# A re-planned order for a graph layer: separate sums for pairs 12 and 13, and zero products that may go into banks about to be set

## The chip, the cores and the metric

The kernel runs on one core of one Trainium2 chip. The metric is the device time of one execution in microseconds (us); several runs of the same kernel give a median. A profile records one execution instruction by instruction; its span runs from the first to the last instruction and is a little shorter than the execution's own time.

## What is computed

A layer of a graph network with 4096 nodes and 64 features. The adjacency matrix, 4096 x 4096 float32 of zeros and ones (64 MB), is nearly all of the traffic.

```python
h = jnp.maximum(_layernorm(x, axis=-1), 0.0)
# _L0_gnn_ref(h, adj, weight, bias), with MAX_NEIGH = 100 and DECAY = 0.5:
support = input @ weight
mask = (adj != 0).astype(support.dtype)
rank = jnp.cumsum(mask, axis=1)
deg = rank[:, -1:]
k = jnp.minimum(deg, float(MAX_NEIGH))
pos = rank - (deg - k)
w = mask * jnp.where(pos > 0, DECAY ** (k - pos), 0.0)
out = w @ support + bias
# result: x + out
```

So a row's last neighbour weighs 1, the one before it 1/2, and so on for at most 100 neighbours: each entry's weight is two to the minus number of neighbours behind it in its row.

## The kernel before

The rows are cut into 32 tiles of 128 rows; a tile (128 x 4096, 2 MB) is also called a unit, and two tiles are a pair (`u`, 16 of them). All tiles go through the same steps:

- `load`: DMA from SP's queue into one of four buffers `a_sb`. The first two tiles and tiles 28 to 31 come in parts.
- `convert` and `flip` (DVE, L563 and L573): the mask as bytes, then a transposition in blocks of 32.
- `totals` (PE, L581, 8 products), `split` (ACT, L589), `suffix` (PE, L602, 9 products), `clamp` (DVE, L608): how many neighbours lie behind each block of columns.
- `place` (PE, L618 and L622, 24 products into four banks): the number of neighbours behind each entry, as an exponent.
- `weigh` (ACT, L636, four to a tile; tiles 29 and 31 in parts): the power of two. For one quarter of tiles 30 and 31 DVE does it instead (`encode` L643, `take` L647).
- `aggregate` (PE, L656): weights times `support`, for a pair of tiles, in eight steps of four products, 32 products in all, summed in a PSUM bank.
- `drain` (ACT L671 or DVE L673) takes the sums out of the bank and adds the bias; `turn_back` (PE, L679) transposes them; `finish` (DVE, L685) adds x; `store` writes.

Ahead of this there is a setup: layer norm and `support` (`turn` to `second`). It fills the first 40 us beside the first tiles.

A bank of sums holds two pairs: `aggregate` takes a new bank at an even pair, and at each pair in `ALONE` (L652). `DRAINS` lists the drains as (group of four tiles, first and last tile in it, whether ACT does it). Before, groups 0 to 6 are drained whole, six of them on ACT and group 6 on DVE; group 7 (pairs 14 and 15, in `ALONE`) in two halves. Half drains share one buffer, `acc_part`, whole ones another, `acc_sb`.

The order of all instructions is fixed by a planner (`plan`, L243), which keeps one queue for each kind of step and picks the next step by the due numbers in `DUE` (L50) and by costs written into `tasks`. It also gives every step its PSUM banks out of eight (`homes`), taking those that come free first, and says how many zero products PE is to run ahead of a step: where it foresees a gap on PE, it asks for products of a zero matrix (`junk`), to keep PE active.

`warm` (L482) issues them. They add zero to a bank of sums that is open: `idle` names its place. `aggregate` sets `idle` to the bank it sums in (L659), and `drain` empties it when that bank is the one drained (L668). While `idle` is empty, `warm` issues nothing. Before any sums exist, the target is a spare bank that each product sets anew. In the loop at the end (L695) `warm` is called ahead of setting `homes` and of the step itself. Each engine then runs its instructions in the planned order.

Of the kernel before, what the change touches and what calls it, by code (L numbers as in the profile page):

```python
# [40 lines left out]

PARTS = {29: ((0, 4), (4, 8)), 31: ((0, 4), (4, 6), (6, 8))}
QUICK = {(30, 3), (31, 3)}
DRAINS = [(g, 0, 4, g < 6) for g in range(7)] + [(7, 0, 2, False), (7, 2, 4, True)]
STORES = [(0, 0, 16), (1, 0, 12), (1, 12, 14), (1, 14, 16)]
NA, NM, NT, NW, BANKS = 4, 4, 4, 2, 8

ALONE = {14, 15}

DUE = {  # L50
    "fetch": [32, 37],
    "load": [35, 38, 39, 40, 36, 34, 33, 29, 31, 21, 20, 16, 25, 14, 18, 17, 15, 12, 13, 11, 6, 2, 1, 3, 7, 5, 9, 8, 4,
    0, 24, 22, 23, 19, 27, 28, 26, 30, 41, 64],
    "constants": [442, 424],
    "order_of": [427],
    "stack": [404],
    "turn": [483, 491, 461, 509, 470, 469, 515, 471],
    "turned": [435, 436, 438, 437, 434, 428, 431, 420],
    "center": [458, 447, 478, 432],
    "square": [441, 443, 492, 466],  # L60
    "relu": [439, 477, 482, 490],
    "spread": [473, 430, 460, 462],
    "support": [419, 97, 465, 459],
    "scale": [500, 454, 449, 507],
    "root": [452],
    "power": [495],
    "count": [474],
    "counted": [444],
    "first": [303, 326, 360, 309],
    "second": [501, 457, 503, 497],  # L70
    "convert": [426, 423, 425, 421, 453, 450, 448, 502, 499, 456, 498, 508, 510, 513, 514, 518, 529, 532, 522, 528, 629,
    631, 623, 626, 591, 617, 618, 538, 604, 594, 600, 553, 599, 593, 560, 584, 587, 564, 554, 578, 576, 570, 550, 551,
    546, 547, 609, 545, 611, 575, 607, 573, 574, 582, 561, 566, 614, 556, 637, 638, 654, 645, 656, 541, 552, 504],
    "flip": [429, 433, 446, 440, 455, 511, 496, 519, 517, 521, 523, 526, 624, 625, 619, 542, 592, 606, 559, 588, 563,
    586, 569, 548, 613, 622, 610, 572, 585, 565, 568, 557, 653, 641, 655, 648, 544, 493, 540, 534],
    "totals": [445, 418, 94, 112, 489, 84, 87, 138, 140, 144, 130, 118, 119, 208, 256, 229, 86, 221, 168, 228, 186, 165,
    145, 164, 197, 179, 49, 45, 63, 71, 73, 479],
    "split": [468, 298, 398, 367, 301, 306, 338, 385, 365, 389, 267, 369, 215, 291, 184, 201, 206, 274, 271, 261, 263,
    401, 335, 319, 295, 293, 322, 379, 381, 414, 356, 357],
    "suffix": [467, 463, 120, 111, 487, 139, 106, 141, 98, 126, 128, 107, 193, 207, 200, 157, 161, 174, 247, 250, 163,  # L80
    212, 205, 198, 177, 236, 55, 66, 69, 76, 51, 650],
    "clamp": [422, 451, 494, 506, 512, 516, 520, 527, 596, 627, 628, 616, 595, 601, 603, 598, 543, 589, 577, 579, 549,
    605, 621, 580, 571, 581, 562, 615, 652, 644, 597, 567],
    "place": [324, 464, 93, 142, 134, 133, 147, 105, 135, 103, 155, 191, 232, 75, 82, 151, 175, 213, 249, 223, 173, 237,
    169, 167, 180, 42, 65, 60, 79, 74, 481, 612],
    "weigh": [505, 216, 243, 342, 321, 325, 328, 361, 312, 307, 302, 355, 366, 387, 373, 374, 386, 364, 354, 399, 396,
    394, 362, 345, 392, 340, 384, 280, 390, 391, 284, 276, 242, 189, 265, 289, 375, 219, 241, 257, 292, 204, 255, 187,
    283, 297, 290, 190, 203, 211, 282, 270, 252, 259, 264, 268, 275, 244, 262, 269, 281, 287, 273, 285, 266, 246, 346,
    334, 279, 288, 327, 278, 332, 260, 402, 339, 337, 348, 314, 331, 341, 299, 351, 336, 311, 320, 310, 376, 308, 318,
    323, 315, 294, 316, 329, 317, 304, 248, 305, 330, 382, 417, 286, 296, 370, 406, 383, 388, 371, 393, 377, 416, 359,  # L90
    368, 350, 358, 378, 395, 352, 372, 405, 412, 397, 347, 353, 333, 349, 403, 413, 343, 415, 407, 410, 344, 411, 409],
    "encode": [533, 524],
    "take": [590, 525, 531, 536],
    "aggregate": [484, 115, 114, 110, 113, 109, 486, 488, 485, 124, 125, 123, 100, 91, 136, 132, 81, 121, 96, 127, 131,
    104, 129, 116, 95, 117, 108, 101, 122, 102, 152, 99, 92, 240, 188, 154, 89, 194, 199, 231, 183, 230, 220, 83, 90,
    85, 78, 77, 159, 153, 148, 150, 222, 158, 162, 166, 235, 214, 234, 245, 300, 182, 258, 227, 253, 225, 178, 195, 218,
    185, 224, 313, 192, 239, 202, 210, 254, 146, 143, 196, 160, 217, 176, 171, 181, 149, 172, 170, 209, 46, 47, 57, 48,
    43, 58, 56, 54, 62, 44, 88, 80, 68, 50, 70, 472, 52, 72, 480, 67, 475, 53, 651, 59, 476, 630, 660, 634, 632, 639,
    647, 657, 649, 658, 640, 642, 643, 633, 636],
    "drain": [363, 277, 251, 272, 400, 380, 608, 583, 408],  # L100
    "turn_back": [137, 233, 156, 226, 238, 61, 661, 659, 646],
    "finish": [530, 602, 558, 555, 620, 635, 537, 539, 535],
    "store": [662, 663, 664, 10],
}
WAIT = 250, 60, 150, 60, 0
PE, DVE, ACT, POOL, SP = range(5)
# [136 lines left out]
def plan():  # L243

    todo, kinds = tasks(), {}
    for key, (f, args, engine, *_) in todo.items():
        kinds.setdefault((engine, f), []).append(key)
    ready, free = {None: 0}, list(FREE)
    landed, taken, order = 0, {p: [] for p in SIZES}, []
    banks = [None] * (BANKS - 1) + read_by(0)  # L250
    while kinds:
        heads = []
        for kind, keys in kinds.items():
            f, args, engine, due, hold, lag, needs, pool = todo[keys[0]]
            if pool and pool[0] in SIZES:
                needs = needs + (taken[pool[0]] + list(pool[1:]))[:-SIZES[pool[0]]][-len(pool) + 1:]
            elif pool:
                needs = needs + [k for _, _, k in sorted((ready[k], i, k) for i, k in enumerate(banks) if k in ready)][:len(pool) - 1]
                if len(needs) < len(todo[keys[0]][6]) + len(pool) - 1:
                    continue  # L260
            if all(r in ready for r in needs):
                heads.append((max([free[engine]] + [ready[r] for r in needs]), due, engine, kind))
        soon, _, engine, _ = min(heads)
        _, at, kind = min((due, at, kind) for at, due, e, kind in heads if e == engine and at <= soon + WAIT[engine])
        key = kinds[kind].pop(0)
        if not kinds[kind]:
            del kinds[kind]
        f, args, _, _, hold, lag, _, pool = todo[key]
        homes = []
        if pool and pool[0] in SIZES:  # L270
            taken[pool[0]] += pool[1:]
        elif pool:
            homes = [i for _, i in sorted((ready[k], i) for i, k in enumerate(banks) if k in ready)][:len(pool) - 1]
            for i, k in zip(homes, pool[1:]):
                banks[i] = k
        if f in ("load", "fetch"):
            lag = max(landed - at, 2450) + dma_ns(f, args)
            landed = at + lag
            lag += late(landed)
        if f in FULL:  # L280
            hold, lag = hold + 95, lag + 95
        ready[key] = at + lag + 60
        free[engine] = at + hold
        order.append((at, hold, engine, f, args, homes))
    spent, end, result = [], 1200, []
    for at, hold, engine, f, args, homes in order:
        idle = 0
        if engine == PE:
            recent = sum(rows for when, rows in spent if when > at - 3400)
            idle = max(0, min(int((at - end) * 0.6) // 110, (4200 - recent) // 256))  # L290
            spent += [(at, rows_of(f, args) + 256 * idle)]
            end = at + hold
        result.append((at, idle, f, args, homes))
    return result
# [3 lines left out]
def kernel(  # L298
# [12 lines left out]
    nc = tc.nc  # L311
    P = 128
# [21 lines left out]
    banks = [ps.tile([P, W], F32, name=f"bank{i}") for i in range(BANKS)]  # L334
    homes = []
# [35 lines left out]
    junk = setup.tile([P, 2 * P], BF16, name="junk")  # L371
# [108 lines left out]
    idle = [banks[BANKS - 1], 2 * P]  # L480

    def warm(n):  # L482
        for i in range(n if idle else 0):
            nc.tensor.matmul(idle[0][:, idle[1]:idle[1] + 2 * P], junk[:, :P], junk, start=not accs, stop=not accs, skip_group_check=True)  # L484

    pxs, ns = {}, {}

# [199 lines left out]
    def store(s):  # L687
# [5 lines left out]
        support, scale, first, second, convert, flip, totals, split, suffix, clamp, place, weigh, encode, take, aggregate,  # L693
        drain, turn_back, finish, store)}
    for at, spare, f, args, given in plan():  # L695
        warm(spare)
        homes[:] = given
        does[f](*args)

    last = {}  # L700
# [34 lines left out]
```

## Time and profile before

| | |
|---|---|
| median of 3 runs | 186.7 us (185.85 to 187.02) |
| the profiled execution | 187.01 us, of which the span is 185.0 us |
| mean granted TensorE clock | 0.98 |
| PE (matmul) busy | 165.2 us (89%) |
| PE weight loads busy | 128.4 us (69%) |
| DVE busy | 153.9 us (83%) |
| ACT busy | 149.5 us (81%) |
| HBM read | 68.19 MB, 374 GB/s over the span |
| weigh (L636) on ACT | 122.7 us, 136 instructions |
| convert (L563) on DVE | 85.7 us, 66 instructions |
| products of aggregate (L656) on PE | 73.2 us, 512 instructions |
| zero products (L484) on PE | 14.7 us, 93 instructions |

The page gives sums over the whole span; three engines are above 80%. Matmuls overlap, so a mean duration of a product (292 ns for L656) is longer than the distance between two: 32 products in a row take about 4 us. A line of the timeline shows the start, the length, the engine, the line of the kernel, the operation with its output and input, how many instructions are merged, and in brackets how long the engine was idle before it and what it waited for. A line of the windows shows a stretch's length, each engine's busy time in it with the number of instructions, the granted TensorE clock (1.00 is full), the share of the DMA engines and GB/s.

### The profile page before, as it was taken

Reading aid. Unit: us, or ns where it says so; the run is one execution under the profiler, and the core shown is the slowest. Engines: PE = TensorE matmul, PEld = TensorE weight load, DVE = VectorE, ACT = ScalarE, POOL = GpSimd, SP = SyncE. Lnnn points to the kernel's source line nnn. Section 1 sums busy time; section 2 is a strip of 40 time slices with the busy share of each in tenths; the row PEclk is TensorE's granted clock in tenths of the full one; section 3 lists DMA queues with packets and bytes.
Section 4 is the critical chain, followed back from the end, with each engine's and each line's share of the span. In section 5 each row is a group of like instructions: output and inputs, shape, how many; then the busy total and the mean of one; then the engine's idle time right before and its main releaser. Section 6 shows DMA issues by size and latency. Waiting matters only on the chain.

```text
span 185.0 us, 4842 instructions
## 1 busy us (share of the span) xinstructions
PE 165.2 (89%) x2087; PEld 128.4 (69%) x2087; DVE 153.9 (83%) x204; ACT 149.5 (81%) x196; POOL 7.7 (4%) x43
## 2 busy tenths in 40 slices
PE   7999987579799999899999899997499999989992
PEld 5857874267586776687868588776277678777891
DVE  6667299999999999898889698888984989998731
ACT  2476912839699999999999999994896999999931
POOL 7810000000000000000000000000000000000000
PEclk9999999999999999999999999999958999999999
DMA  6999999999999999999999999999999999960020
GB/s 225 420 415 436 429 425 418 441 407 446 414 436 418 427 425 418 436 429 425 425 422 432 418 429 432 418 432 425 429 422 420 413 416 416 414 267 0 4 87 28
DMA packets 6807, 69.55 MB, mean 376 GB/s; under 512 B 898, under 2 KB 1154, under 8 KB 2178
## 3 DMA queue, kind: packets, MB, share of 16 engines
q1 hardware_dynamic: 6786, 69.24, 89.1%
q8 instruction: 16, 0.26, 0.6%
q14 instruction: 5, 0.04, 0.1%
HBM read 68.19 MB, written 1.05 MB: 374 GB/s over the span
## 4 chain that ended last, share of the span: by engine, by line
ACT 29%; PE 26%; DMA 19%; DVE 16%; issue 8%; SPq 0%; ACTq 0%; DVEq 0%
ACT wk L636 23%; DMA a_sb<-in_adj_dram 19%; PE bank L656 15%; DVE m L563 8%; ACT sums L589 4%; PE bank L602 4%; DVE mt L573 3%; PE bank L679 3%; PE bank L622 2%; PE bank L581 2%; PE bank L618 2%; DVE behind L608 1%; DVE wk L532 1%; DVE hr L542 1%; ACT acc_sb L671 1%
## 5 line engine op out<-in xcount | busy, mean ns | idle before, releaser
L636 ACT ACTIVATE wk<-bank 128x1024 fp32r<-128x1024 uint8 (+2 forms) x136 | 122.7, 1067 | 7.9 <-PE bank L622 6.3
L563 DVE TENSOR_SCALAR m<-a_sb 128x2048 uint8<-128x2048 f32 (+1 forms) x66 | 85.7, 1345 | 14.5 <-DMA a_sb<-in_adj_dram 14.3
L656 PE MATMUL bank<-wk,hr 128*128 128x256 f32 x512 | 73.2, 292 | 3.5 <-DVE hr L542 2.5
L656 PEld LDWEIGHTS bank<-wk,hr 128*128 128x128 f32 x512 | 64.4, 192 | 10.3 <-issue 5.0
L573 DVE STREAM_TRANSPOSE mt<-m 128x1024 f32<-128x1024 f32 (+2 forms) x40 | 40.5, 1022 | 0.4
L589 ACT ACTIVATE sums<-bank 128x512 f16<-128x512 uint8 x32 | 21.6, 685 | 7.2 <-PE bank L581 7.2
L608 DVE TENSOR_SCALAR behind<-bank,excess 128x256 f16<-128x256 f32 x32 | 14.8, 466 | 4.4 <-PE bank L602 4.1
L602 PEld LDWEIGHTS <-far 128*128 128x128 f16 x224 | 17.7, 99 | 0.9
L602 PE MATMUL bank<-sums,far 128*128 128x224 f16 (+6 forms) x224 | 18.1, 222 | 0.0
L618 PE MATMUL bank<-behind,where 32*128 32x256 f16 x256 | 14.5, 277 | 3.9 <-DVE behind L608 1.9
L484 PE MATMUL bank<-junk 128*128 128x256 bf16 x93 | 14.7, 299 | 1.2 <-DVE junk L372 1.2
L581 PE MATMUL bank<-mt,band 128*32 128x256 f16 x256 | 13.3, 284 | 2.4 <-DVE mt L573 1.7
L622 PE MATMUL bank<-mt,tri 32*32 32x512 f16 x512 | 14.4, 403 | 0.0
L602 PE MATMUL bank<-sums,near 128*128 128x256 f16 x32 | 9.0, 280 | 4.4 <-ACT sums L589 3.8
L484 PEld LDWEIGHTS <-junk 128*128 128x128 bf16 x93 | 9.0, 106 | 4.8 <-issue 2.0
L618 PEld LDWEIGHTS <-where 32*128 32x128 f16 x256 | 4.7, 92 | 9.8 <-issue 7.4
L581 PEld LDWEIGHTS <-band 128*32 128x32 f16 x256 | 4.5, 95 | 7.9 <-issue 3.8
L622 PEld LDWEIGHTS <-tri 32*32 32x32 f16 x512 | 4.4, 88 | 6.9 <-issue 6.9
L602 PE MATMUL bank<-sums,rest 128*128 128x256 f16 x32 | 8.8, 276 | 0.0
L495 ACT ACTIVATE wk<-bank 64x512 f32<-64x512 f32 x8 | 4.3, 587 | 4.9 <-PE bank L491 4.9
L685 DVE TENSOR_TENSOR xr<-bank,xr 128x256 f32<-128x256 f32 (+1 forms) x9 | 3.5, 389 | 5.6 <-PE bank L679 5.6
L679 PE MATMUL bank<-both,acc_sb 128*128 128x64 f32 x56 | 7.5, 277 | 0.6 <-ACT acc_sb L671 0.6
(95 smaller groups left out, 86.2 us busy)
## 6 DMA issues: line engine op xcount, KB each, us to landing
a_sb<-in_adj_dram SPq DMA_DIRECT2D x26, 2048.0 KB, 16.8
a_sb<-in_adj_dram SPq DMA_DIRECT2D x10, 1024.0 KB, 12.7
a_sb<-in_adj_dram SPq DMA_DIRECT2D x4, 512.0 KB, 14.5
xr<-in_x_dram SPq DMA_DIRECT2D x2, 512.0 KB, 4.8
out_dram<-xr SPq DMA_DIRECT2D x1, 512.0 KB
out_dram<-xr SPq DMA_DIRECT2D x1, 384.0 KB, 2.7
out_dram<-xr SPq DMA_DIRECT2D x2, 64.0 KB, 1.6
w<-in_L_gnn_weight_dram SPq DMA_DIRECT2D x2, 16.0 KB, 9.4
```

The lines of the kernel that those rows point to most:

```text
L484: nc.tensor.matmul(idle[0][:, idle[1]:idle[1] + 2 * P], junk[:, :P], junk, start=not accs, stop=not accs, skip_group_check=True)
L563: nc.vector.tensor_scalar(words[n][:, k0 * P:k1 * P, :].rearrange("p (h q) e -> p h e q", q=P), tiles[t][:, (h0 + k0) * W:(h0 + k1) * W].r ...
L573: nc.vector.transpose(to[:, h0:h1], m_v.rearrange("p (h c l) -> p h c l", c=4, l=SUB))
L581: nc.tensor.matmul(tot[SUB * c:SUB * (c + 1), r], band[:, SUB - 12 - 4 * a:2 * SUB - 12 - 4 * a], masks[t][:, c, r, a], start=(a == 0), st ...
L589: nc.scalar.activation(sums8[t][:, :, r], pts.pop((n, "n")).bitcast(U8).rearrange("p (i f) -> p f i", f=4)[:, :2, r], AF.Copy, bias=-136.0)
L602: nc.tensor.matmul(o, l, m, start=(k == 0), stop=(k == len(todo) - 1), skip_group_check=True)
L608: nc.vector.tensor_scalar(behind[n][:, r], pts.pop((n, "s"))[:, r], excess, float(MAX_NEIGH), op0=ALU.subtract, op1=ALU.min)
L618: nc.tensor.matmul(vs[n, j][:, h0:h1, a, :], where[q, a, :], behind[n][q, r], start=(a == 0), stop=False, skip_group_check=True)
L622: nc.tensor.matmul(vs[n, j][SUB * c:SUB * (c + 1), h0:h1], tri[q, q], masks[t][q, c, r, :].rearrange("p (h r) a -> p h a r", r=SUB), start ...
L636: nc.scalar.activation(to[:, :, :, j, :], v[:, :2, x], AF.Exp, scale=-LN2, bias=-38.0 * LN2)
L656: nc.tensor.matmul(accs[g][:, at:at + 2 * P], hr[:, h * 4 + e, :, :].rearrange("p s d -> p (s d)"), wts[u][:, s, 2 * h + a].rearrange("p i ...
L679: nc.tensor.matmul(pts["o", d][:, k, :], sums[d][:, k * P:(k + 1) * P], both, start=True, stop=True)
```

## The change

Three edits. The lists: pairs 12 and 13 no longer share a bank of sums but have separate ones, as pairs 14 and 15 had, and group 6 is drained in two halves, the first on ACT and the second on DVE. The due numbers: nearly all are new, so that the order of steps and the banks that they get differ throughout. The zero products: `homes` is now set before `warm` is called, and when `idle` is empty, `warm` writes into the first bank given to the step that follows, with products that set the bank anew.

```diff
-DRAINS = [(g, 0, 4, g < 6) for g in range(7)] + [(7, 0, 2, False), (7, 2, 4, True)]
+DRAINS = [(g, 0, 4, g < 6) for g in range(6)] + [(6, 0, 2, True), (6, 2, 4, False)] + [(7, 0, 2, False), (7, 2, 4, True)]
...
-ALONE = {14, 15}
+ALONE = {12, 13, 14, 15}
...
 DUE = {
-    "fetch": [32, 37],
-    "load": [35, 38, 39, 40, 36, 34, 33, 29, 31, 21, 20, 16, 25, 14, 18, 17, 15, 12, 13, 11, 6, 2, 1, 3, 7, 5, 9, 8, 4,
+    "fetch": [35, 39],
+    "load": [36, 40, 38, 37, 34, 33, 32, 30, 31, 21, 20, 15, 25, 13, 17, 18, 16, 11, 14, 12, 7, 1, 0, 3, 8, 4, 6, 5, 9,
...
     def warm(n):
-        for i in range(n if idle else 0):
-            nc.tensor.matmul(idle[0][:, idle[1]:idle[1] + 2 * P], junk[:, :P], junk, start=not accs, stop=not accs, skip_group_check=True)
+
+        to = idle or [banks[i] for i in homes[:1]] + [0]
+        for i in range(n if len(to) > 1 else 0):
+            keep = bool(idle and accs)
+            nc.tensor.matmul(to[0][:, to[1]:to[1] + 2 * P], junk[:, :P], junk, start=not keep, stop=not keep, skip_group_check=True)
...
     for at, spare, f, args, given in plan():
-        warm(spare)
         homes[:] = given
+        warm(spare)
         does[f](*args)
```

The part of the planned order that the prediction speaks of, for the steps around pair 9 on PE and around unit 21 on ACT (a step's first number is its tile or its pair):

```
PE before:  place 20 | totals 21 | aggregate 9, steps 0 to 7 | totals 22 | suffix 21 | turn_back 4 | suffix 22 | place 21 | place 22 | totals 23 | suffix 23
PE after:   place 20 | suffix 21 | aggregate 9, 0 to 2 | totals 22 | place 21 | aggregate 9, 3 to 5 | suffix 22 | aggregate 9, 6 and 7 | totals 23 | place 22
ACT before: weigh 20 (4) | split 21 | drain 4 | split 22 | weigh 21
ACT after:  split 21 | weigh 20 (4) | split 22 | weigh 21 (3) | drain 4 | split 23 | weigh 21 (1)
```

And at the end, on PE, from pair 12 on:

```
PE before:  ... place 31 | aggregate 14, 5 to 7 | turn_back 6 | aggregate 15 | turn_back 7 | turn_back 8
PE after:   aggregate 12, 0 to 3 | suffix 27 | aggregate 12, 4 and 5 | totals 28 | place 27 | suffix 28 | aggregate 12, 6 and 7 | place 28 | totals 29 | turn_back 6 | aggregate 13
            ... totals 31 | place 30 | turn_back 7 | suffix 31 | aggregate 14, 2 and 3 | place 31 | aggregate 14, 4 to 7 | aggregate 15 | turn_back 8 | turn_back 9
ACT after:  ... weigh 27 (3) | drain 6 | weigh 27 (1) | split 29 | weigh 28
```

## The prediction

> **What bounds the kernel now.** I read four views. First the slices of the page: the granted TensorE clock and the traffic of the loads.
>
> ```profile
> PEclk9999999999999999999999999999958999999999
> GB/s 225 420 415 436 429 425 418 441 407 446 414 436 418 427 425 418 436 429 425 425 422 432 418 429 432 418 432 425 429 422 420 413 416 416 414 267 0 4 87 28
> ```
>
> A slice is 185.0/40 = 4.6 us. The reader is to see two things: the loads run at one rate until slice 36, so no engine starves them; and the clock falls once, in slices 30 and 31. The windows around the fall (PE, PEld, DVE, ACT, POOL busy us, clock, DMA) and the timeline of PE there say why:
>
> ```profile
> 127.90:131.30 3.40, 1.89 (x56) 0.93 (x54) 3.40 (x6) 1.03 (x2) 0.00 (x0) 1.00 1.02 434
> 129.90:133.30 3.40, 1.41 (x48) 0.56 (x33) 3.40 (x4) 3.03 (x4) 0.00 (x0) 1.00 1.00 424
> 133.30:140.10 6.80, 6.43 (x55) 4.55 (x55) 4.90 (x5) 5.79 (x8) 0.00 (x0) 0.50 1.01 426
> ```
>
> ```profile
> 121.67 4.04 PE L656 MATMUL bank<-wk,hr 128*128 128x256 f32 x32 [0.20 <-ACT wk L636]
> ...
> 129.41 0.40 PE L618 MATMUL bank<-behind,where 32*128 32x256 f16 x8 [1.11 <-DVE behind L608]
> ...
> 131.35 0.41 PE L581 MATMUL bank<-mt,band 128*32 128x256 f16 x8 [0.44 <-ACT wk L636]
> 133.67 0.37 PE L602 MATMUL bank<-sums,near 128*128 128x256 f16 x1 [1.91 <-ACT sums L589]
> ```
>
> PE is idle for 1.11, 0.44 and 1.91 us, the clock is halved for 6.8 us, and what PE does in that time (6.43 us busy) takes twice as long: about 3.2 us of PE lost. ACT and DVE pay too. From their timelines:
>
> ```profile
> 130.27 2.85 ACT L636 ACTIVATE wk<-bank 128x1024 fp32r<-128x1024 uint8 x3 [3.36 <-PE bank L622]
> ...
> 143.68 0.60 ACT L589 ACTIVATE sums<-bank 128x512 f16<-128x512 uint8 x1 [1.01 <-PE bank L581]
> ```
>
> ```profile
> 141.36 0.48 DVE L608 TENSOR_SCALAR behind<-bank,excess 128x256 f16<-128x256 f32 x1 [2.59 <-PE bank L602]
> ```
>
> Last the chain of waits: from 144.4 to 162.4 us it lies on ACT, then on PE without a gap to 180.5. In the stretch 140.1 to 162.4 PE is busy 21.2, ACT 21.3 and DVE 20.0 of 22.3 us: three nearly full engines, none with room to make up 3 us, and the end carries the debt. The loads set the floor: the last is issued at 150.9 and takes 15.0 us, so it lands at 165.9, but its conversion on DVE begins at 167.81, 1.9 us late, and the end comes 19 us after the landing.
>
> **What the Trainium skill says.** "TensorE: Matmul & The Clock Gate", Part 1: The HAM clock gate, gives two states, half and full rate, and says that the array falls to half after an idle window of about 3.4 us that is free-running. The trace agrees on the two states (0.50 and 1.00) and on the grain (6.8 us is two such windows); but no 3.4 us were wholly idle, PE was busy 41% (1.41 of 3.40) in the last window before the fall. The stretch 31.5 to 36.5 us was 57% busy and kept its clock. Its section Architectural detail has ACT and DVE as strict FIFOs, which the order of the trace bears out. "PSUM — Partial Sum Buffer", The four PSUM rules: a first product of a group clears the bank's bits, so a junk product into a bank that the next step sets anew leaves nothing behind; no run shown tests that.
>
> **The change, part by part.** I set the two kernels' orders of instructions against each other.
>
> *Zero products.* The planner of before asks for 108; the program has 93. The 15 that are missing are the 2, 3 and 10 ahead of place 21, totals 23 and suffix 23, exactly the three gaps above: drain 4 had emptied `idle`, so warm did nothing. After asks for 106 and issues 106; 16 of them (6, 5, 3 and 2) go to the bank of the step behind them, at units 6, 4/5, 16 and 29. Each costs 0.12 us (16 in 1.92 at 37.49), and a first one waits for its bank's last reader, for which the step itself would wait anyway. They lie in gaps of PE: cost taken as 0. Were the cover gone at units 16 and 29, 5 x 0.12 = 0.6 us.
>
> *The order.* Before, ACT runs split 21 only after the last weigh of unit 20, and PE runs all 32 products of pair 9 (4.04 us) ahead of suffix 21: the 3.36 us of ACT come from that. After, split 21 stands ahead of the four weighs of unit 20, suffix 21 ahead of pair 9, and place 21 after its third step of eight. So the stall should go even without zero products: ACT has 4 x 0.93 = 3.7 us of weighs in hand while PE needs 0.63 (suffix) + 0.72 (place) + 12 x 0.125. At the front DVE reaches the last "second" some 1.1 us later (two flips of 1.2 more, one conversion of 1.3 less ahead of it), but the splits of units 3 and 4 are done by then, so ACT doesn't pause for them after unit 2 as it does at 46 to 48.5 us. I count 0: the loads run on in either case, and ACT has until 126 us to catch up, as it does now. SP's and POOL's orders are the same in both, and no load moves.
>
> *Pairs 12 and 13.* One DVE drain of 0.74 becomes one of 0.47 on ACT and one of 0.47 on DVE, and one finish of 0.42 two of 0.29: ACT +0.47, DVE -0.11. Eight products of turn_back stay eight, but they leave the stretch after the last place: now 12 products of sums, 8 of turn_back and 32 of sums follow it, afterwards 48 of sums. A new wait comes with it: in the order, pairs 12 and 13 both sum in bank 92, so PE's turn_back 6 and all of pair 13 stand behind drain 6, which stands on ACT behind three weighs of unit 27. From place 27 ACT needs 3 x 0.93 + 0.47 = 3.3 us to end it; PE has suffix 28 (0.63), a quarter of pair 12 (8 x 0.125 = 1.0), place 28 (0.72), two zero products (0.24) and totals 29 (0.34) to do, 2.9. So 0.4 us of wait at least, if ACT isn't late; the bounds are 0 and 3.3 (PE has nothing ready). I take 0.2 at the end, since loads pace that stretch.
>
> *The sum, by the tail.* With the clock kept, DVE has its 2.59 us back and meets the last landing. From 165.9: conversion 0.73, two flips 0.74, at 167.4; totals 31 (0.34) 167.7; clamp 30 (0.48) is done at 167.9 and place 30 (0.72) at 168.6; turn_back 7 (0.5) 169.1; suffix 31 (0.63) 169.7; DVE meanwhile is in "encode" (1.22, from 168.6), so clamp 31 (0.48) ends at 170.3; 8 products of sums run to 170.75 and place 31 ends at 171.45. Then 48 products at 4.01/32 = 0.125: 6.0, at 177.5. ACT's nine part weighs (3.24) are through at 174.7, ahead of need. Before, the same point is 180.36: 2.9 us gained, less the 0.2: **2.7 us**. What follows (two half drains, one after the other through one buffer, and the store) is 4.6 us in both. Span 185.0 - 2.7 = 182.3; the profiled execution took 187.01 and so takes 184.3. It stands 0.3 above the median of the runs, 186.7; I forecast the median, 186.7 - 2.7 = **184.0**. If PE were never late for unit 31, its place would end at 167.4 + 0.34 + 0.60 (split) + 0.63 + 0.48 + 0.72 = 170.1, 1.3 better: 182.7 is about the floor.
>
> **Rivals.** *Same, the loads and DVE keep the debt* (0.13). DVE is 1.9 us late at the end; if that is its own load (20.0 of 22.3 us busy from 140 to 162) and not the 2.59 us stall, then 2.9 - 1.9 - 0.2 = 0.8 is gained: 185.9. For it: DVE also waits 0.9 for suffix 25 at 150.5, at full clock. Against: it still waited for loads at 136.13, so it was on time until the fall.
> *The clock falls elsewhere* (0.11). Other stretches have thin PE work, the front above all, and the zero products there are set out differently (16 ahead of place 1, 16 ahead of totals 4). A fall early is made good before 126 us; one after 120 costs what it does now: 186.7, between 186 and 187.5.
> *Slower: the wait for drain 6* (0.10). If ACT is late, pair 13 waits up to 3.3 us with PE empty. At 1.9 us of PE idle, the gap after which the clock fell before, it takes the clock with it: 2.0 + 3.2 (6.4 us at half) = 5.2 in the last 25 us, where nothing makes it good; -2.7 + 5.2 gives 189.2. Against: ACT has 0.6 us of spare in each 4.9 us of load pace (4 x 0.93 + 0.5).
> *The change does not do what it says*: "its own bank" is not a further bank for pairs 12 and 13, as said; the wait is costed above.
>
> **How the numbers follow.** Within 1% (186.7 x 0.01 = 1.9 us, about what a measurement here can tell) means 184.8 to 188.6. The main case has 0.66, its own range 182.7 to 184.9, nearly all faster. The two middle rivals, 0.24, are "same"; the last, 0.10, is slower. Range 182.6 to 187.6: floor of the tail below, the clock rival's upper end above; out of it stay the slow rival and little else.
>
> **What would show it.** Right: no slice below 9 in the clock row behind the first; ACT's idle time of 3.36 ahead of unit 21's weighs gone; the last conversion beginning within 0.5 us of 165.9; place 31 ending near 171.5. Wrong: a clock of 0.5 anywhere after 120 us; a wait of "PE bank L656" or the turn_back for the half drain over 1.9 us; DVE as late as now at the last load.

## The result, and the profile after

The changed kernel takes 184.55 us (median of 4 runs, 184.51 to 184.59), the kernel before 186.86 in the same set: a ratio of 0.9888 with a 95% interval of 0.9849 to 0.9928. The forecast was 184.0 us, in a range of 182.6 to 187.6. The profiled execution took 184.57 us, with a span of 182.6 against 185.0. In the later sets the kernel before has medians of 186.01 to 186.49 us, from 22 to 27 executions each, so the 2.3 us between these two medians may be some tenths too much; the kernel after was not run again beside them. In all that follows, an execution over 1.5% longer than the fastest of its kernel is in the median and the range, but not in the ratio.

The page of the kernel after, the granted clock and the traffic in 40 slices:

```profile
PEclk9999969999999999999999999999999999999997
GB/s 228 418 406 441 424 434 415 438 413 438 413 434 420 429 424 431 424 427 431 427 431 420 431 413 434 409 445 409 445 413 438 395 422 415 414 374 95 85 7 29
```

The loads run as before. The fall in slices 30 and 31 is gone; in its place there is a short one in slice 6, at 23 us, which had not been foreseen. The 7 in the last slice is a fall from about 180.4 us on, when PE's last product is through, and costs nothing. The windows of the kernel after, over the stretches that were shown of before, and over the new fall (stretch; busy PE, PEld, DVE, ACT, POOL; clock; DMA; GB/s):

```profile
127.90:131.30 3.40, 3.40 (x44) 2.85 (x42) 2.95 (x4) 3.40 (x5) 0.00 (x0) 1.00 1.01 429
129.90:133.30 3.40, 3.40 (x57) 2.58 (x56) 2.98 (x4) 3.40 (x6) 0.00 (x0) 1.00 0.96 410
133.30:140.10 6.80, 6.11 (x82) 5.10 (x82) 6.38 (x8) 6.80 (x9) 0.00 (x0) 1.00 1.00 422
...
23.30:26.70 3.40, 3.40 (x20) 3.36 (x18) 3.12 (x12) 0.00 (x0) 0.00 (x0) 0.52 1.05 448
```

PE has no gap from 128 to 133 us, where it had been busy 56% and 41% of the two stretches, and ACT, which had stood for 3.36 us there, is busy throughout. The tail, on the timeline of PE after (start, length, engine, line, output and input, count, idle before):

```profile
158.15 0.40 PE L621 MATMUL bank<-behind,where 32*128 32x256 f16 x8 [1.03 <-DVE behind L611]
158.48 0.45 PE L625 MATMUL bank<-mt,tri 32*32 32x512 f16 x16
158.86 0.39 PE L487 MATMUL bank<-junk 128*128 128x256 bf16 x2
159.36 0.41 PE L584 MATMUL bank<-mt,band 128*32 128x256 f16 x8
159.71 0.66 PE L682 MATMUL bank<-both,acc_part 128*128 128x64 f32 x4
...
171.92 6.11 PE L659 MATMUL bank<-wk,hr 128*128 128x256 f32 x48
177.87 0.55 PE L682 MATMUL bank<-both,acc_part 128*128 128x64 f32 x4
```

The last conversion on DVE, before and after:

```profile
167.81 0.73 DVE L563 TENSOR_SCALAR m<-a_sb 128x1024 uint8<-128x1024 f32 x1
```

```profile
166.45 0.73 DVE L566 TENSOR_SCALAR m<-a_sb 128x1024 uint8<-128x1024 f32 x1
```

After, it begins about 0.15 us after its load has landed (issued at 151.1, 15.2 us to landing); before, it was 1.9 us late. From 172 us the chain of waits is the 48 products of sums and then the drains, as the prediction's sum has it. Ahead of that the chain has changed: before, it lay on ACT from 144 to 162 us; after, it lies on two loads, from 119.3 to 136.0 and from 139.2 to 156.3 us. Of the whole chain, loads are 30% (19% before) and ACT is 17% (29% before).

### The profile page after: what moved, and what is told of

Read it like the earlier page. It is cut to its first block, busy times and chain, and to the rows that moved or that the text cites. A ratio compares the mean times of both kernels' runs of the same rounds, so it can differ in the third digit from the quotient of the medians.

```text
span 182.6 us, 4869 instructions
## 1 busy us (share of the span) xinstructions
PE 165.6 (91%) x2100; PEld 128.9 (71%) x2100; DVE 154.3 (85%) x205; ACT 149.7 (82%) x197; POOL 8.0 (4%) x43
## 4 chain that ended last, share of the span: by engine, by line
PE 31%; DMA 30%; ACT 17%; DVE 15%; issue 4%; SPq 0%; DVEq 0%; ACTq 0%
DMA a_sb<-in_adj_dram 30%; PE bank L659 17%; ACT wk L639 15%; DVE m L566 7%; PE bank L605 5%; DVE mt L576 3%; PE bank L625 2%; PE bank L621 2%; PE bank L682 2%; PE bank L584 2%; ACT sums L592 2%; DVE wk L535 1%; DVE behind L611 1%; DVE hr L545 1%; ACT acc_sb L674 1%
## 5 line engine op out<-in xcount | busy, mean ns | idle before, releaser
L639 ACT ACTIVATE wk<-bank 128x1024 fp32r<-128x1024 uint8 (+2 forms) x136 | 121.4, 1035 | 3.4 <-PE bank L625 3.1
L659 PEld LDWEIGHTS bank<-wk,hr 128*128 128x128 f32 x512 | 63.3, 188 | 10.9 <-issue 5.7
L592 ACT ACTIVATE sums<-bank 128x512 f16<-128x512 uint8 x32 | 20.8, 661 | 6.8 <-issue 4.2
L487 PE MATMUL bank<-junk 128*128 128x256 bf16 x106 | 16.0, 296 | 1.4 <-DVE junk L372 1.2
L584 PE MATMUL bank<-mt,band 128*32 128x256 f16 x256 | 12.8, 280 | 3.9 <-DVE mt L576 3.7
L487 PEld LDWEIGHTS <-junk 128*128 128x128 bf16 x106 | 10.3, 106 | 4.7 <-issue 1.6
L542 ACT ACTIVATE hr<-wk 128x512 fp32r<-128x512 f32 x4 | 2.4, 628 | 8.9 <-DVE wk L535 8.9
```

The source lines that it names most:

```text
L487: nc.tensor.matmul(to[0][:, to[1]:to[1] + 2 * P], junk[:, :P], junk, start=not keep, stop=not keep, skip_group_check=True)
L584: nc.tensor.matmul(tot[SUB * c:SUB * (c + 1), r], band[:, SUB - 12 - 4 * a:2 * SUB - 12 - 4 * a], masks[t][:, c, r, a], start=(a == 0), st ...
L592: nc.scalar.activation(sums8[t][:, :, r], pts.pop((n, "n")).bitcast(U8).rearrange("p (i f) -> p f i", f=4)[:, :2, r], AF.Copy, bias=-136.0)
L639: nc.scalar.activation(to[:, :, :, j, :], v[:, :2, x], AF.Exp, scale=-LN2, bias=-38.0 * LN2)
L659: nc.tensor.matmul(accs[g][:, at:at + 2 * P], hr[:, h * 4 + e, :, :].rearrange("p s d -> p (s d)"), wts[u][:, s, 2 * h + a].rearrange("p i ...
```

## The experiments

Twelve runs of kernels. All times are medians; each ratio is to the kernel before, run beside it on the same chip.

**The rule alone.** The order of before, with the new `warm`:

```diff
-        for i in range(n if idle else 0):
+        to = idle or [banks[i] for i in homes[:1]] + [0]
+        for i in range(n if len(to) > 1 else 0):
...
-        warm(spare)
         homes[:] = given
+        warm(spare)
```

> The order, sums and drains of before, with the new rule for zero products alone: the 15 products that before left out are issued, 10 of them ahead of suffix 23 once the weigh that reads their bank is through. Theory A (the fall of the clock costs the time): the clock holds at 1.00 from 120 us on, PE gets 3.2 us back and DVE its wait of 2.59 us, but ACT's stall of 3.36 us ahead of unit 21's weighs stays; 185.2 us, between 184.5 and 186.0. Rival B (the gain is the order's and the tail's; the fall is absorbed): 186.7 us, clock 1.00 or not.

Measured: 184.95 us (184.69 to 185.08), before 186.34; ratio 0.9915 (0.9881 to 0.9949). The granted clock of this kernel in 40 slices, and the timeline of PE where the gaps had been:

```profile
PEclk9999999659999999999999999999999999999999
```

```profile
128.53 0.38 PE L487 MATMUL bank<-junk 128*128 128x256 bf16 x2
129.71 0.40 PE L621 MATMUL bank<-behind,where 32*128 32x256 f16 x8 [0.81 <-DVE behind L611]
...
131.65 0.49 PE L487 MATMUL bank<-junk 128*128 128x256 bf16 x3 [0.45 <-ACT wk L639]
132.07 0.41 PE L584 MATMUL bank<-mt,band 128*32 128x256 f16 x8
132.57 1.25 PE L487 MATMUL bank<-junk 128*128 128x256 bf16 x10
133.97 0.27 PE L605 MATMUL bank<-sums,near 128*128 128x256 f16 x1 [0.16 <-ACT sums L592]
```

The 15 products are there, and the gap of 1.91 is filled. The three still wait for the bank's reader (0.45 us), as the step would. ACT's stall is there too:

```profile
130.57 2.87 ACT L639 ACTIVATE wk<-bank 128x1024 fp32r<-128x1024 uint8 x3 [3.28 <-PE bank L625]
```

The clock holds after 120 us. So in this order the fall is worth 1.4 us by the medians (2.0 by the spans of the two profiled executions, 183.0 and 185.0), of the 3.2 us of PE that were lost in it, and theory A is borne out: 15 products that compute nothing, with nothing else changed. This execution has a fall of two windows of its own, in slices 8 and 9 (32 to 41 us). It took 184.94 us; the four others with a mean clock near 0.99 took 184.69 to 184.99, so that one cost nothing that shows.

**The order alone.** The kernel after with the old `warm`: the reverse of the edit above.

> The order, sums and drains of after, with the old rule: 16 zero products (6 at place 6, 5 at pair 2, 3 at suffix 16, 2 at totals 29) are not issued. Theory A: the order alone closes the gaps of 1.11, 0.44 and 1.91 us, the clock holds from 120 us on, 184.5 us within 0.4. Rival (the products carry it): without the 3 and 2 late ones the clock falls near 100 or near 158 us, 3.2 us of PE lost, 186.5 us or more.

Measured: 184.85 us (184.14 to 186.91), before 186.34; ratio 0.9901 (0.9863 to 0.9939). The granted clock in 40 slices:

```profile
PEclk9999969699999969999999999999999999999999
```

No fall after 120 us, as expected of the order; besides the early one two more, from about 33 and 64 us. Either half of the change takes the fall at 133 us away, and the two don't add up. Without the execution of 186.91 us the median is 184.57, that of after (184.55), and 1.8 us below this set's before, where the rule alone gains 1.4. So with the order in place, the medians leave nothing for the rule to add. What the rule may do is steady the kernel: its executions spread over 2.8 us here and go with their mean clock (184.14 and 184.24 us at 0.988, 184.57 at 0.981, 185.12 and 185.23 at 0.972, 186.91 at 0.963), where after's four lie within 0.1 us at 0.985 and 0.986.

**One bank for pairs 12 and 13.** First with `DRAINS` and `ALONE` as before in the kernel after, and one entry each taken from three lists of due numbers:

```diff
-DRAINS = [(g, 0, 4, g < 6) for g in range(6)] + [(6, 0, 2, True), (6, 2, 4, False)] + [(7, 0, 2, False), (7, 2, 4, True)]
+DRAINS = [(g, 0, 4, g < 6) for g in range(7)] + [(7, 0, 2, False), (7, 2, 4, True)]
...
-ALONE = {12, 13, 14, 15}
+ALONE = {14, 15}
```

> After, with pairs 12 and 13 in one bank of sums and group 6 drained whole by DVE; the planned order is the same up to the totals of unit 29, then moves a little. Theory A: the clock holds, and the split drain is worth 0 to 0.5 us: 184.6 to 185.1. Rival B (the tail is the gain): 8 products of turn_back and the drain come back into the last stretch, 1 us and more: 185.6 us or more.

Measured: 186.0 us (185.8 to 186.49), ratio 0.9983 (0.9967 to 0.9998): the rival's number. But the planner had moved the tail, too: ACT waits 2.20 us for place 30, which now stands behind suffix 31, and PE 0.82 us for a drain ahead of pair 15. So the order was held fixed in a second kernel, with the merged drain put into after's very list of steps (parts of it):

```diff
+    DRAINS, ALONE = DRAINS[:6] + [(6, 0, 4, False)] + DRAINS[8:], {14, 15}
...
+    for at, spare, f, args, given in order:
+        if f in ("drain", "turn_back", "finish"):
+            if args[0] == 6:
+                continue
+            args = (args[0] - (args[0] > 6),)
...
```

> After, in after's very order, but pairs 12 and 13 sum in one bank, the first half drain with its turn_back and finish is gone, and the second stands for the whole group (0.74 us on DVE, 8 products). Theory A (the 186.0 us of the kernel with one bank came from its re-planned tail: turn_back ahead of suffix 31, place 30 behind it, a wait of PE for a drain): here 4 more products of turn_back ahead of suffix 31, 0.3 to 0.6 us over after: 184.9 to 185.2 us. Rival B (separate sums are the gain themselves): 186.0 us.

Measured: 184.69 us (184.46 to 184.93), before 186.01; ratio 0.9924 (0.9897 to 0.9951). Its span is after's, 182.6. That is below the 184.9 to 185.2 us expected, and far from the rival's 186.0. The separate sums make no difference here that can be told (0.14 us to after's median, with a spread of 0.5). The first kernel's loss goes with its re-planned tail: 1.3 us between the two medians, 1.0 if each is taken against the before run beside it.

**The early fall.** Zero products between the spreads of the setup, in the kernel after:

```diff
     def spread(n):
...
+        warm(8 if n > 1 else 0)
         for b in range(4 * n, 4 * n + 4):
```

> After, with 8 zero products ahead of each of the last two spreads of the setup, to keep the clock from falling at 23 us. If long runs of products with two columns leave the clock's monitor idle: the early fall goes (1.00 in all slices behind the first). Theory A: an early fall is made good by 120 us, 184.5 us within 0.3. Rival C (ACT, which is hardly idle from 42 us on, carries the early loss to the end): 1 to 2 us faster, 182.5 to 183.5.

Measured: 184.69 us (184.6 to 184.79), ratio 0.9903 (0.9873 to 0.9934). In the profiled execution the clock is at 1.00 from end to end; in the five others its mean is 0.985 to 0.991, after's own being 0.985 and 0.986, so it isn't shown that the products keep the fall away. The profiled one answers the question all the same: no fall, and the same span, 182.6. Until 29.7 us ACT waits for DVE in any case, for 8.6 us, and rival C falls.

**A clamp behind a load.** On DVE, flip of the first part of tile 29 behind its conversion, clamp 28 ahead of the second part's conversion (the list of steps, not code):

```diff
-convert 32 | convert 33 | clamp 28 | flip 32 | flip 33
+convert 32 | flip 32 | clamp 28 | convert 33 | flip 33
```

> After, with one swap on DVE: flip of the first part of tile 29 right behind its conversion, and clamp 28 ahead of the conversion of the second part, which waits for its load. Theory A (from 158 us on the end is PE's, and PE lost 1.03 us there to a clamp that stood behind a load): place 28 starts 1 us earlier and totals 29 by 0.4 us; 184.15 us, between 183.9 and 184.5. Rival (weights of unit 27 on ACT, through at 159.5 us, hold pair 13 anyway): 184.55 us.

Measured: 184.57 us (184.18 to 185.02), ratio 0.992 (0.989 to 0.9949). In its profiled execution place 28 starts at 157.16 instead of 158.15 and the last sums at 171.59 instead of 171.92; that one took 184.24 us. Over six executions nothing is left that can be told from after. The median is the rival's; whether for the rival's reason was not looked into.

**PE's time near 130 us.** Two fillers ahead of place 22 in the kernel after, 60 products of 2 columns (shown) or 30 of 256:

```diff
+        if (f, args) == ("place", (22,)):
+            for i in range(60):
+                nc.tensor.matmul(idle[0][:, idle[1]:idle[1] + 2], junk[:, :P], junk[:, :2], start=False, stop=False, skip_group_check=True)
         does[f](*args)
```

> After, with 60 zero products of 2 columns ahead of place 22, at about 130 us. If products of few columns count as idle for the clock, as at 23 us in after: the clock falls to 0.50 within 4 us of them and stays there for some 7 us. Theory A: their own time on PE (some 3.6 us) and the fall (3 us) reach the end almost whole: 3 us above the twin with wide products, 189 us or more. Rival B (a fall is absorbed): within 1 us of the twin.

> After, with 30 zero products of 256 columns ahead of place 22, at about 130 us: 30 x 0.12 = 3.6 us of PE, and the clock holds. Theory A: PE has about 1 us of idle time to give between 130 and 160 us, so 1.5 to 3.6 us above after: 186 to 188 us. Rival (PE is not the bound before 158 us): 184.6 to 185.2 us.

Measured: thin 185.6 us (185.27 to 186.74), ratio 0.9977 (0.9952 to 1.0001); wide 187.39 us (187.17 to 189.62), ratio 1.0097 (1.0053 to 1.0141). The thin kernel was forecast to be 3 us slower than its twin and is 1.8 us faster. The twins weren't equal in time, so their difference says nothing: the thin products took 1.65 us together, not the 3.6 expected, the wide ones 3.45.

```profile
131.07 1.65 PE L703 MATMUL bank<-junk 128*128 128x2 bf16 x60
```

```profile
133.39 3.45 PE L703 MATMUL bank<-junk 128*128 128x256 bf16 x30
```

Read singly they do tell something. Wide, inside the 186 to 188 us forecast: 3.45 us of PE at a full clock cost 187.39 - 184.55 = 2.8, so PE has some 0.6 us to give at 130 us. Thin: the clock fell behind them, windows of that kernel:

```profile
131.00:134.00 3.00, 2.92 (x97) 2.32 (x89) 2.65 (x2) 1.30 (x4) 0.00 (x0) 1.00 1.03 437
134.00:137.40 3.40, 3.40 (x22) 3.23 (x22) 1.19 (x3) 3.40 (x4) 0.00 (x0) 0.52 0.99 414
```

That execution took 186.57 us; 1.65 us of filler and half of 3.2 us are 3.25 us of PE lost, for 2.0 us of time. The kernel's other executions were not traced, and whether the fall is in them is open. This one has two falls, in slices 8 and 30, and a mean clock of 0.982. Six others have 0.991, which leaves about 0.009 x 183.6 x 2 = 3.3 us at half clock, one such fall, and took 185.54 to 185.93 us.

**Before, again.** Unchanged, for its own spread.

> The kernel before, unchanged, for a second profiled execution: its executions lie between 185.4 and 187.5 us at mean clocks of 0.96 to 0.99, so that the fall near 133 us seems not to be the same in each. Theory A: the faster an execution, the shorter its fall after 120 us: at 185.4 to 186.0 us a fall of one window (3.4 us) or none there, at 187 us one of two windows. Rival: the fall near 133 us is there in full at 185.5 us too, and the spread comes from elsewhere.

> As the run before it: a third profiled execution of the kernel before. Theory A: its time goes with its half-clock time after 120 us (none: 185.4; 3.4 us: 186; 6.8 us: 187).

Measured: 186.58 us (185.74 to 187.06), and 186.51 in the single run. The profiled ones took 186.81 and 186.51 us; both have the gap of 1.91 us ahead of suffix 23 and a fall of 6.8 us. In the second it begins at 132.3 us, inside the gap, and is over at 139.2, and there is another fall of two windows in slices 8 and 9, which cost nothing that shows. No execution near 185.4 us was traced, but the mean clocks of 119 executions of before are on record. In 14 of them, from three chips, it is 0.991, which leaves about 0.009 x 183.7 x 2 = 3.3 us at half clock in the whole execution, one window; they took 185.40 to 185.86 us. The 20 at 0.980, as in the profiled one with its two windows at 133 us, took 186.75 to 187.52. That agrees with theory A. But the mean clock alone doesn't give the time (at 0.976 it is 185.68 to 186.24): where in the execution those falls lie isn't on record.

**No zero products once sums exist**, in the kernel after:

```diff
-        for i in range(n if len(to) > 1 else 0):
+        for i in range(n if len(to) > 1 and not accs else 0):
```

> After, without the 50 zero products that it issues once a bank of sums is open or has been. Theory A (after's order leaves no gap of PE after 120 us, and falls before that are made good): no fall after 120 us, 184.2 to 184.9 us, with one or two more falls between 38 and 100 us. Rival (the products hold the clock): falls near 123 and 158 us, 186 us or more.

Measured: four executions from 185.04 to 188.72 us, the profiled one 186.66. The profiled one has no fall after 120 us, as theory A had it, but its time is 1.8 us over the forecast's upper end, and only the fastest came near it (0.1 us over). The four falls between 23 and 68 us weren't made good; they begin at about 24, 34, 51 and 64 us, and after has the first of them alone. Windows of this kernel, then of after, 45 to 120 us and 120 to 165:

```profile
45.00:120.00 75.00, 66.51 (x913) 51.02 (x913) 64.98 (x67) 67.61 (x83) 0.00 (x0) 0.95 1.01 426
120.00:165.00 45.00, 42.80 (x598) 33.97 (x602) 42.13 (x47) 44.62 (x55) 0.00 (x0) 1.00 0.99 413
```

```profile
45.00:120.00 75.00, 69.92 (x981) 53.29 (x974) 68.03 (x68) 70.17 (x86) 0.00 (x0) 1.00 1.01 426
120.00:165.00 45.00, 42.23 (x598) 33.05 (x598) 41.16 (x47) 44.08 (x56) 0.00 (x0) 1.00 0.99 412
```

At 45 us ACT is as far as in after (24.65 us busy, 24.84 in after), so the loss goes with the falls at 51 and 64 us and not with the first two: ACT comes to 120 us with 2.6 us less done, and has 0.4 us of idle time left up to 165 us in which to make it good. The span is 2.0 us longer.

That suggests an account: ACT's busy time from 45 to 165 us against the span.

| kernel | ACT busy, 45 to 165 us | span |
|---|---|---|
| before (three executions) | 112.25, 112.34, 112.73 | 185.0, 184.8, 184.5 |
| after | 114.25 | 182.6 |
| rule alone | 114.29 | 183.0 |
| order alone | 113.51 | 183.2 |
| one bank, same order | 114.65 | 182.6 |
| no early fall | 114.05 | 182.6 |
| clamp ahead of the load | 114.65 | 182.2 |
| no late zero products | 112.22 | 184.6 |
| thin filler | 112.05 | 184.6 |
| wide filler | 111.36 | 187.4 |
| one bank, re-planned | 114.10 | 184.2 |

Two microseconds of ACT go with about two of span. DVE's busy time does much the same (before 107.2, after 109.2, no late zero products 107.1, thin filler 107.3, wide filler 104.4), so the table shows that what isn't done by 165 us is paid after it, and not that ACT is the engine that decides. Two kernels stand out. The last one's ACT waits after 165 us. In the wide filler's profiled execution (189.4 us, 2.0 over its median) the clock fell more in the setup, and ACT came to 45 us with 22.3 us done, where the others have 24.3 to 24.8. The account would explain, too, why the rule alone nearly suffices: before's order brings ACT to 120 us with 72.6 us done, after's with 70.2, so the stall of 3.3 us only spends a lead of 2.4.

**The account, tested.** Before's order with the rule, and the stall planned away (the numbers, not code; the rule's edit is as above):

```diff
 # due numbers of unit 21
-split 401, suffix 212, clamp 605, place 237
+split 0, suffix 0, clamp 0, place 0
```

> The order of before with the new rule for zero products, and the due numbers of split, suffix, clamp and place of unit 21 set to 0, so that the planner puts split 21 behind the first weigh of unit 20 and suffix 21 and place 21 inside pair 9; what follows is re-planned. Theory C (the end is set by ACT's idle time between 45 and 165 us: 2 us more of busy time went with 2.2 us less of span in the runs so far): ACT keeps its lead of 2.4 us at 120 us over after and loses the stall of 3.3 us, busy 115 us or more from 45 to 165 us, span 182 us or less, 184.0 us or less. Rival D (without the stall ACT runs into the loads and waits for them instead): no more busy than after, 114.3 us, 184.5 us or more.

Measured: 187.47 us (186.93 to 190.46), before 186.2; ratio 1.0056 (1.0038 to 1.0074): far above theory C's 184.0 us. It lies within rival D's bounds (184.5 us or more, ACT no more than 114.3 us busy), but not for D's reason, which was a wait for the loads. The stall is gone from 127 us, and the re-plan put a longer one elsewhere. Timeline of ACT, and windows, of this kernel:

```profile
144.91 0.69 ACT L670 ACTIVATE acc_sb<-bank,bias_sb 128x512 f32<-128x512 f32 x1 [4.19 <-PE bank L655]
```

```profile
45.00:165.00 120.00, 110.69 (x1553) 84.64 (x1545) 109.19 (x115) 111.83 (x136) 0.00 (x0) 1.00 1.00 421
```

A drain stands ahead of a split on ACT and waits 4.19 us for its pair's last sums. The clock is at 1.00 throughout this execution, and its span is 185.5 us with 111.83 us of ACT: it fits the account (2.4 us less ACT than after, 2.9 us more span; DVE, with 109.19 us, is as far as in after), and a full clock alone doesn't make a fast execution. But the stall was moved and not removed, so the account's forecast wasn't tested: the saving that it promised was not reached, and whether the loads would have swallowed it stays open.

## Why the prediction was right

- **The clock fall as the cost, 3.2 us of PE.** Shown by the rule alone: the same order, the gap filled, 1.4 us by the medians and 2.0 by the spans. The cost was the right one, but not all of it reached the end.
- **The order closes the gaps without zero products.** Forecast ("the stall should go even without zero products"), and shown by the order alone. The prediction took the new rule's products at nothing, and beside the new order nothing is what they are worth in the medians. It didn't forecast that the rule alone, in the old order, would bring most of the gain: the stall of 3.36 us on ACT, which it set beside the fall, stays there (3.28 us), in a kernel only 0.4 us over after's median.
- **The tail, where the forecast's 0.55 us went.** Forecast: place 31 ends at 171.45, the last product at 177.5, then 4.6 us. Measured: 171.99, 178.03, 4.6. The sums after the last place took 6.04 us against 6.0. The 0.5 us missing is ahead of place 31: DVE reached the last conversion 0.5 us later than its landing was taken to be (166.45 for 165.9), of which 0.4 is the load itself, that came later. Against it stand the 0.2 us of the next point, which were subtracted and did not come: 182.6 of span against 182.3. The other 0.3 is the step from the profiled execution to the median, carried over from before (187.01 and 186.7); after has none (184.57 and 184.55).
- **The wait for drain 6, 0.2 us.** Mis-sized and misplaced: PE's turn_back shows no wait for it at 159.71, nor at 159.38 in the kernel with the clamp moved. PE did wait 1.03 us for clamp 28, which stood on DVE behind a conversion that waited for its load. That wait the prediction didn't see; moving it away was not worth anything that shows in the median.
- **The separate sums.** The prediction's tail has 8 products of turn_back fewer and 4 of sums more in the last stretch, without a figure of their own. In the same order, one bank or two differ by 0.14 us, not told from nothing.
- **The front, counted at 0, and "a fall early is made good".** The first is half right: the early fall costs nothing (no early fall), but ACT does 2.4 us less from 45 to 120 us than before, which the removed stall pays for. The second holds for falls up to 41 us, which cost nothing that shows (rule alone, before again); those at 51 and 64 us went with 2.6 us less of ACT and 2.0 us more of span in the one traced execution (no late zero products).
- **The signs.** "No slice below 9" was wrong: slice 6, of which more below, and the last, after PE's work, which literally is also the sign of being wrong "anywhere after 120 us". The last conversion was to begin within 0.5 us of 165.9 and missed that by 0.05. ACT's idle time went, as forecast.
- **The rival of DVE's debt** falls: DVE is 0.15 us late at the end, at almost the same load. Its lag was the fall's: with the rule alone its last conversion begins at 166.20. **The slower rival** needed an empty PE at 158 us; it was empty for 1.03 us, for another reason, and the clock held. The 1.91 us that the rival took as the gap at which the clock falls isn't that: in the second profile of before the clock fell 0.7 us into that gap.

## What to carry to other kernels

Where three engines are nearly full and the loads set the pace, look for the stretch in which the work loses its lead: here gaps on PE, followed by 6.8 us at half clock with no slack behind them, took 3.2 us of PE and cost 1.4 to 2.0 us at the end, while falls before 41 us cost nothing that shows. Before moving work, see whether a filler for that gap is planned and lost on a side condition; here 15 products gave 1.4 us, where the whole new order gave 1.8 against the same before. And with a planner that re-plans everything after an edit, hold the list of steps fixed when one edit is to be measured: by the medians, the same merged drain cost 1.45 us over after in a new plan and 0.14 in the old one.

## What the runs showed of the hardware that was not expected

A busy PE can lose its clock. Ahead of the fall at 23 us in the kernel after, PE is busy without a break, with products of two columns:

```profile
20.07 2.74 PE L514 MATMUL bank<-ones,wk 128*128 128x2 f32 x24
```

The setup of before issues 16 of these, other work, and 16 more, and kept its clock there. 60 thin products at 131 us were followed by a fall at 134. So it may be columns streamed that count for the clock, rather than time busy; that isn't shown, and the record has a case against a simple rule. In the profile of the thin filler the same 24 products run from 19.71 us, and no fall follows them until 31.7 us:

```profile
19.90:23.30 3.40, 3.40 (x35) 3.38 (x36) 1.51 (x2) 1.14 (x2) 0.00 (x0) 1.00 1.00 429
23.30:26.70 3.40, 3.40 (x34) 3.02 (x34) 3.13 (x12) 0.00 (x0) 0.00 (x0) 1.00 1.00 424
```

With 8 products of 256 columns between the groups, one traced execution kept its clock, which with this case beside it shows little.

Nor does the share of busy time decide by itself. In the second profile of before the clock fell at 132.3 us after 3.4 us in which PE was busy 1.90 (56%); in the kernel after it stayed at 1.00 with 1.63 of 3.40 us (48%) from 30.1 to 33.5 us.

Nor is it the same in each execution: before's mean clock took values such as 0.96, 0.98 and 0.99 from run to run. Where a fall comes from in a single execution is thus open; what it costs depends on when it comes.
